# A feed-forward stage put in the order of its source: all engines by hand, gate sums on DVE, left sums two steps later, w3's sums over four steps

## The chip, the cores and the metric

The kernel runs on one core of a Trainium2 chip. The metric is device time in microseconds (us), the median of several executions. The engines are named as the profile names them: PE (TensorE), DVE (VectorE), ACT (ScalarE), POOL (GpSimd), SP (SyncE, which here issues the transfers). Each engine works through its own queue in order, and waits on semaphores for the others.

## The reference

The kernel computes one transformer layer in float32 for 16 sequences of 128 rows with 1024 features: cross-attention with a residual, and a gated feed-forward network (FFN) with a residual, each behind a layer norm. Cut to what matters:

```python
x = x + cross_attention(layernorm(x), ctx, mask)
xn = layernorm(x)
x12 = jnp.einsum('bsk,mk->bsm', xn, w12) + b12      # w12: 2048 x 1024
x1, x2 = jnp.split(x12, 2, axis=-1)
x4 = jax.nn.silu(x1) * x2
out = x + jnp.einsum('bsm,nm->bsn', x4, w3) + b3    # w3: 1024 x 1024
```

The kernel calls the residual stream `x1` (the `x` of the last line), and the gated product `h` (the `x4` here).

## The kernel before

Both products of the FFN are made with fewer multiplications than the plain form. The first product, F here, is a two-level seven-product scheme. The outer level splits the operands into 2 x 2 quarters and forms seven products, in the order `OUTER = (1, 2, 3, 6, 5, 7, 4)`; for each of them there are four groups g of rows of w12 (each holds gate rows and value rows), so that there are 28 *steps*, `STEPS = [(g, i) for i in OUTER for g in range(4)]`: i=1 is steps 0 to 3, i=2 steps 4 to 7, i=3 steps 8 to 11, i=6 steps 12 to 15, i=5 steps 16 to 19, i=7 steps 20 to 23 and i=4 steps 24 to 27. In each step the function `seven` does the inner level: seven inner products of four chunks each, in the order `INNER = (1, 5, 6, 7, 2, 3, 4)`, accumulated in PSUM. The second product, G, is a scheme of 26 products on 4 x 4 blocks (`bilinear`), done for four groups of columns, G0 to G3.

Each product needs sums made by other engines:

- *Outer sums.* `outer_sum` makes the left operand of outer products 5, 6, 3 and 7 on POOL from quarters of w12 (128 x 1024 elements each, lines L836, L839, L841, L845). A sum is kept in DRAM (`keep_sum`) and read back (`load_sum`) two steps ahead of its use.
- *Inner left sums.* `inner_left` makes four sums of 128 x 256 elements for each step on POOL, one step ahead (L289, tiles named L).
- *Right sums.* `outer_right` and `inner_right` make the sums of the right operand on DVE (128 x 1024 each, tiles X); `made` says at which step and product.
- *u1 and u3.* In each step ACT copies the first inner product out of PSUM (L271), and DVE adds it to the later ones (u1 at L274, u3 at L276). PE's inner product 3 adds to the bank that u3 reads, and product 4 to the bank of product 7, so PE waits there if DVE is late.
- *The state.* `done` adds each outer product to running sums u, v and w of each group, which are kept as two tiles of 128 x 1024 per group; `spill` and `unspill` move them to DRAM and back. When a block of the result is complete, `finish` puts it on the list `due`: gates get their silu on ACT (L901), values are multiplied with the gate on DVE (L895), and the product is stored to `hT_dram` by SP (L898). `settle_due` works off the list after each inner product.
- *For G.* `w3_R.advance` loads blocks of w3 and makes their sums on DVE in the last steps of F; `load_left` reads `hT` back, `load_x1` loads four tiles of x1 and b3, spread over all partitions; `add_b3` adds b3 to x1 on DVE (L1035).

What happens when is written out by hand as a plan: `at(n, j, fn, ...)` calls a function in step n after inner product j. In the kernel before, that plan fixes the order for PE only (`tc.manual_schedule(engines={PE})`); the order of the instructions on DVE, ACT, POOL and SP is chosen by the framework's scheduler from its own costs. All loads and stores are issued by SP, with at most eight outstanding: each one waits for the eighth before it. Large tiles share a pool of 44 units of 512 KB, smaller temporaries one of 14[...].

Of the kernel before, what the change touches and what calls it, by code (L numbers as in the profile page):

```python
# [15 lines left out]
AX = mybir.AxisListType  # L16
PSUM = bass.MemoryType.PSUM
# [100 lines left out]
def xattn_ffn_kernel(  # L118
# [33 lines left out]
    ctx.enter_context(tc.manual_schedule(engines={mybir.EngineType.PE}))  # L152
# [732 lines left out]

    gate, held, due = {}, {}, []
# [30 lines left out]
    def step(n):  # L917
        g, i = STEPS[n]

        def done(rc, s, ps):  # L920
# [8 lines left out]
            elif i == 2:  # L929
                t = temp([512], f"C11_{g}_{r}{c}")  # L930
                nc.vector.tensor_add(t, u, ps)
                if s is not None:
                    nc.gpsimd.tensor_add(t, t, s)
                finish(g, 0, 0, r, c, t)
            elif i == 6:
                nc.vector.tensor_add(u, u, ps)
                if s is not None:
                    nc.vector.tensor_add(u, u, s)
            elif i == 5:
                nc.vector.tensor_add(w, u, ps)  # L940
                if s is not None:
                    nc.vector.tensor_add(w, w, s)
                nc.gpsimd.tensor_add(v, v, w)
                finish(g, 0, 1, r, c, v)
            elif i == 7:
                if s is None:
                    nc.vector.tensor_add(w, w, ps)
                    nc.vector.tensor_add(u, u, ps)
                else:
                    t = temp([512], f"M7_{g}_{r}{c}")  # L950
                    nc.vector.tensor_add(t, s, ps)
                    nc.vector.tensor_add(w, w, t)
                    nc.gpsimd.tensor_add(u, u, t)
                finish(g, 1, 1, r, c, w)
            else:
                nc.vector.tensor_add(u, u, ps)
                if s is not None:
                    nc.gpsimd.tensor_add(u, u, s)
                finish(g, 1, 0, r, c, u)
# [7 lines left out]
    for n, (g, i) in enumerate(STEPS):  # L967
# [3 lines left out]
        else:  # L971
# [3 lines left out]
        if i == 1:  # L975
            at(n - (g > 0), 1 if g == 0 else 6, load_quarter, g, 1, 0)
            at(n - (g > 0), 2 if g == 0 else 7, load_quarter, g, 1, 1)
            at(n, 4 if g == 0 else 1, outer_sum, g, 5)
            at(n, 5 if g == 0 else 2, outer_sum, g, 6)
            for k in (5, 6):  # L980
                at(n + 1, 1, keep_sum, g, k)
        if i == 2:
            at(n - 2, 3, load_sum, g, 6)
            at(n, 1, outer_sum, g, 3)
            at(n + 1, 1, keep_sum, g, 3)
        if i == 6:
            at(n - 2, 3, load_quarter, g, 0, 0)
            at(n - 2, 4, load_quarter, g, 1, 0)
            at(n, 1, outer_sum, g, 7)
            at(n + 1, 1, keep_sum, g, 7)  # L990
# [6 lines left out]
        for k, s in ((6, "u"), (5, "v")):  # L997
            if i == k:
                at(n - 1, 2, unspill, g, s)
# [15 lines left out]
    made(5, [(4, 7), (5, 7), (6, 7), (7, 7)], sums((12, 3), (12, 6), (13, 4), (14, 4)))  # L1015
    made(6, [(7, 3), (8, 2), (8, 6), (9, 2)], sums((9, 5), (10, 2), (10, 5), (11, 2)))
    made(7, [(9, 7), (10, 7), (11, 4), (11, 6)], sums((16, 4), (17, 4), (18, 4), (19, 4)))
    made(4, [(13, 6), (14, 6), (15, 3), (15, 6)], sums((20, 4), (21, 4), (22, 4), (23, 4)))
# [15 lines left out]
    def add_b3(k, i):  # L1034
        nc.vector.tensor_add(x1_in[k][i], x1_in[k][i], last["b3"])  # L1035
# [29 lines left out]
    for j in range(1, 8):  # L1065
        for e in range(3):
            at(N - 3 + e, j, w3_R.advance, 7 * e + j)
    at(N - 3, 3, load_left, 0)
    at(N - 2, 2, load_x1, 0)
    for j in range(4):  # L1070
        at(N - 1, 1 + j, lambda j=j: A[0].advance(j))
        at(N - 1, 4 + j, add_b3, 0, j)
# [27 lines left out]
    stream.add(*(step(n) for n in range(N)))  # L1100
    stream.finish()
    settle_due()
# [63 lines left out]
```

## Time and profile before

| | |
|---|---|
| median of the runs | 1217.68 us (1216.41 to 1219.34, three runs) |
| profiled execution | 1217.48 us |
| its span | 1215.5 us |
| granted PE clock, mean | 0.986 |
| PE busy | 1167.4 us (96%) |
| DVE busy | 840.5 us (69%) |
| POOL busy | 678.1 us (56%) |
| ACT busy | 330.7 us (27%) |
| bytes moved | 183.86 MB, 151 GB/s over the span |

The span is the time between the first and the last instruction of the profiled execution; the 2 us around it belong to the launch. "Busy" is the time in which an engine had an instruction under way. The page divides the span into 40 slices of about 30 us and gives a digit for each. Queries of the trace give, for a stretch of time, the busy time of each engine, what each wait of an engine was for, and the groups of instructions with the same line and shape. F runs from about 647 us to 999 us, G to the end.

### The profile page before, as it was taken

To read this page: it belongs to the slowest core of one execution; us is meant where nothing else is said; L and a number is where in the kernel's file an instruction comes from. 1 tells how busy PE (TensorE), PEld (TensorE's weight loads), DVE (VectorE), ACT (ScalarE), POOL (GpSimd) and SP (SyncE) were. 2 spreads that over 40 slices of the span, in tenths; PEclk is the share of its full clock that TensorE was granted. 3 is DMA by queue.
4 is the path that set the end of the run, shared out by engine and by line. 5 is a ranking of instruction groups with operands and counts; after the bars stand their busy time and mean duration, and the time that the engine had idled before them with its cause. 6 is when DMAs were issued, how large, how long until landed. Compare 5 with 4: busy or idle time off the path is not lost.

```text
span 1215.5 us, 13386 instructions
## 1 busy us (share of the span) xinstructions
PE 1167.4 (96%) x4276; PEld 542.1 (45%) x4276; DVE 840.5 (69%) x1211; ACT 330.7 (27%) x1308; POOL 678.1 (56%) x584
## 2 busy tenths in 40 slices
PE   7999999999999999999999987999996998899998
PEld 3444445445444545444454433444442443344443
DVE  4742368977687888888343685647687769989762
ACT  0000044555445454544342211110011111111210
POOL 6753256745457556647153695537179455547645
PEclk9999999999999999999999998999998999899999
DMA  9535342221215513153576772368143351252411
GB/s 367 204 111 200 102 158 87 88 87 53 87 53 191 183 68 116 47 185 136 217 272 238 292 255 107 122 255 349 52 159 127 112 199 70 95 200 103 165 70 69
DMA packets 60900, 183.86 MB, mean 151 GB/s; under 512 B 6560, under 2 KB 10656, under 8 KB 60832
## 3 DMA queue, kind: packets, MB, share of 16 engines
q1 hardware_dynamic: 59248, 178.81, 40.3%
q10 hardware_dynamic: 1584, 4.21, 0.9%
q8 instruction: 34, 0.56, 0.2%
q14 instruction: 34, 0.28, 0.1%
HBM read 121.14 MB, written 61.87 MB: 151 GB/s over the span
## 4 chain that ended last, share of the span: by engine, by line
PE 80%; POOL 8%; DVE 6%; DMA 3%; issue 2%; ACT 1%; SPq 0%; POOLq 0%; DVEq 0%; ACTq 0%
PE F_b L187 21%; PE Q_b L187 18%; PE O_b L187 16%; PE G_b L187 14%; PE pt L547 4%; POOL L L289 3%; PE s L514 3%; PE o L559 2%; POOL A_S L289 2%; DMA b_sb<-in_b_dram 1%; POOL wm L436 1%; DVE w_R L289 1%; PE xt L653 1%; DMA S6r<-S_dram 1%; DVE wo_T L231 1%
## 5 line engine op out<-in xcount | busy, mean ns | idle before, releaser
L541 POOL TENSOR_TENSOR p<-p,inv 128x512 f32<-128x512 f32 x128 | 136.3, 1087 | 168.2 <-DVE inv L538 128.9
L532 ACT ACTIVATE p<-s,nmax 128x128 f32<-128x128 f32 x512 | 181.4, 406 | 176.2 <-DVE nmax L526 168.7
L187 PE MATMUL F_b<-X_T,L 128*128 128x512 f32 x304 | 137.5, 599 | 2.2 <-POOL L L289 2.2
L532 ACT ACTIVATION_READ_ACCUMULATOR p<-s,nmax 128x1 f32 x512 | 126.0, 246 | 0.0
L187 PE MATMUL G_b<-w_R,A_L 128*128 128x512 f32 x256 | 116.1, 598 | 6.4 <-DVE A_L L289 6.4
L523 DVE SCALAR_TENSOR_TENSOR s<-s,mr,drop 128x512 f32<-128x512 f32 x128 | 90.3, 750 | 24.9 <-PE s L514 24.9
L549 DVE COPY pT<-pt 128x512 f32<-128x512 f32 x128 | 84.3, 675 | 18.1 <-PE pt L547 17.6
L547 PEld LDWEIGHTS pt<-ident,p 128*128 128x128 f32 x512 | 63.6, 141 | 69.8 <-issue 63.7
L187 PEld LDWEIGHTS F_b<-X_T,L 128*128 128x128 f32 x304 | 57.8, 192 | 74.7 <-issue 66.6
L187 PE MATMUL F_b<-xnT,L 128*128 128x512 f32 x128 | 64.5, 623 | 18.6 <-DVE F_u L276 18.6
L526 DVE TENSOR_REDUCE nmax<-s 128x4 f32<-128x512 f32 x128 | 81.7, 678 | 0.0
L187 PEld LDWEIGHTS G_b<-w_R,A_L 128*128 128x128 f32 x256 | 49.1, 192 | 68.8 <-issue 67.1
L547 PE MATMUL pt<-ident,p 128*128 128x128 f32 x512 | 76.9, 273 | 2.4 <-issue 2.4
L289 POOL TENSOR_TENSOR x<-x,G_n 128x512 f32<-128x512 f32 x36 | 51.5, 1454 | 39.2 <-DVE G_n L352 18.3
L289 POOL TENSOR_TENSOR x<-x,G_c 128x512 f32<-128x512 f32 x36 | 53.9, 1511 | 34.7 <-ACT G_c L370 30.4
L370 ACT COPY G_c<-G_b 128x512 f32<-128x512 f32 x52 | 30.3, 585 | 143.3 <-PE G_b L187 130.7
L187 PE MATMUL O_b<-wo_T,O_S 128*128 128x512 f32 x128 | 61.7, 601 | 0.0
L187 PE MATMUL O_b<-wo,O_S 128*128 128x512 f32 x128 | 61.6, 601 | 0.0
L187 PE MATMUL Q_b<-xT,wq 128*128 128x512 f32 x128 | 60.0, 596 | 0.0
L187 PE MATMUL Q_b<-xT_T,A_S 128*128 128x512 f32 x128 | 59.9, 598 | 0.0
L187 PE MATMUL Q_b<-xT,A_S 128*128 128x512 f32 x128 | 59.7, 598 | 0.0
L187 PE MATMUL O_b<-wo,OTr 128*128 128x512 f32 x112 | 55.6, 601 | 0.2 <-DMA OTr<-OT_dram 0.2
(220 smaller groups left out, 2091.5 us busy)
## 6 DMA issues: line engine op xcount, KB each, us to landing
w<-in_w_dram SPq DMA_DIRECT2D x36, 512.0 KB, 5.5
xT<-in_xT_dram SPq DMA_DIRECT2D x16, 512.0 KB, 6.7
xs<-in_x_dram SPq DMA_DIRECT2D x16, 512.0 KB, 6.0
xp<-in_x_dram SPq DMA_DIRECT2D x16, 512.0 KB, 6.6
x_dram<-xp SPq DMA_DIRECT2D x16, 512.0 KB, 2.6
xn_dram<-xn SPq DMA_DIRECT2D x16, 512.0 KB, 2.9
xnr<-xn_dram SPq DMA_DIRECT2D x16, 512.0 KB, 5.8
h<-hT_dram SPq DMA_DIRECT2D x16, 512.0 KB, 4.4
```

What stands on the lines that cost most here:

```text
L187: nc.tensor.matmul(ps, lhsT, rhs, start=start and i == 0, stop=stop and i == len(pairs) - 1, skip_group_check=True,)
L231: eng.tensor_sub(t[e], a()[e], b()[e])
L289: (eng.tensor_add if op == "+" else eng.tensor_sub)(out, a, b)
L370: nc.scalar.copy(t, ps)
L514: nc.tensor.matmul(ps[gl][:, j, :], QT[T, c, gh * 2 + j // 2][rows, j % 2, toks], KT[T, c][rows, gh, toks], start=True, stop=True,)
L523: nc.vector.scalar_tensor_tensor(s, s, rstd, drop.unsqueeze(1).to_broadcast([P, HPG, S]), ALU.mult, ALU.add,)
L526: nc.vector.tensor_reduce(nmax[:, e], s, AX.X, ALU.max, negate=True)
L532: nc.scalar.activation(p[:, j, :], ps[gl][:, j, :], AF.Exp, bias=nmax[:, e, j : j + 1], accum_out=total[:, e, j : j + 1],)
L541: nc.gpsimd.tensor_mul(p, p, inv[:, e].unsqueeze(2).to_broadcast([P, HPG, S]))
L547: nc.tensor.transpose(pt[:, j, :], p[:, j, :], ident)
L549: nc.vector.tensor_copy(pT, pt)
L559: nc.tensor.matmul(o[ds(gl * DH, DH), :, :], V[T, c][:, i, ts(gh * GL + gl, DH)], pTs[gl], start=True, stop=True,)
```

## The change

Six things change, all in F or at its border with G.

1. Inside F, the order of the source holds for all five engines instead of PE alone. Outside it nothing changes.
2. For i=2, the sum of the inner result and the gate's running sum (`C11`) is added on DVE instead of POOL.
3. Outer sums 5 and 6 are made two steps after their group's step of i=1 instead of in it, from quarters loaded one step after it. Outer sum 3 is made two steps ahead of its step of i=3, from sum 6 and a quarter loaded for it, and outer sum 7 two steps ahead of its step of i=7; neither goes through DRAM any more.
4. For i=5, w and v are formed from the product alone on DVE (one of the four blocks of w by a copy on ACT), and POOL adds u to the whole tiles of v (one step before) and of w (one step after); v is read back one step earlier.
5. The sums of the right operand for i=5, 6, 7 and 4 are made at other steps and products.
6. The first 20 of w3's blocks and sums are spread over four steps, five in each, instead of three with seven. x1 and b3 are loaded in step 25 after product 5 instead of step 26 after product 2, and for the first group of columns POOL adds b3 in step 26 instead of DVE in step 27.

```diff
+    def add_u(g, s):
+        for r in range(2):
+            nc.gpsimd.tensor_add(state[g, s][r], state[g, s][r], state[g, "u"][r])
...
                 nc.vector.tensor_add(t, u, ps)
                 if s is not None:
-                    nc.gpsimd.tensor_add(t, t, s)
+                    nc.vector.tensor_add(t, t, s)
                 finish(g, 0, 0, r, c, t)
...
             elif i == 5:
-                nc.vector.tensor_add(w, u, ps)
-                if s is not None:
-                    nc.vector.tensor_add(w, w, s)
-                nc.gpsimd.tensor_add(v, v, w)
+                if s is None:
+                    nc.vector.tensor_add(v, v, ps)
+                    nc.scalar.copy(w, ps)
+                else:
+                    nc.vector.tensor_add(w, s, ps)
+                    nc.vector.tensor_add(v, v, w)
                 finish(g, 0, 1, r, c, v)
...
         if i in (1, 2, 4):
             at(n - 2, 2, load_quarter, g, i // 2 // 2, (i + 1) // 3)
-        else:
+        elif i in (6, 5):
             at(n - 2, 2, load_sum, g, i)
...
         if i == 1:
-            at(n - (g > 0), 1 if g == 0 else 6, load_quarter, g, 1, 0)
-            at(n - (g > 0), 2 if g == 0 else 7, load_quarter, g, 1, 1)
-            at(n, 4 if g == 0 else 1, outer_sum, g, 5)
-            at(n, 5 if g == 0 else 2, outer_sum, g, 6)
+            for e, (R, K) in enumerate(((1, 0), (1, 1), (0, 0))):
+                at(n + 1, 4 + e, load_quarter, g, R, K)
+            at(n + 2, 2, outer_sum, g, 5)
+            at(n + 2, 3, outer_sum, g, 6)
             for k in (5, 6):
-                at(n + 1, 1, keep_sum, g, k)
-        if i == 2:
-            at(n - 2, 3, load_sum, g, 6)
-            at(n, 1, outer_sum, g, 3)
-            at(n + 1, 1, keep_sum, g, 3)
-        if i == 6:
-            at(n - 2, 3, load_quarter, g, 0, 0)
-            at(n - 2, 4, load_quarter, g, 1, 0)
-            at(n, 1, outer_sum, g, 7)
-            at(n + 1, 1, keep_sum, g, 7)
+                at(n + 3, 1, keep_sum, g, k)
+        if i == 3:
+            at(n - 3, 2, load_quarter, g, 0, 1)
+            at(n - 3, 3, load_sum, g, 6)
+            at(n - 2, 1, outer_sum, g, 3)
+        if i == 7:
+            at(n - 3, 2, load_quarter, g, 0, 0)
+            at(n - 3, 3, load_quarter, g, 1, 0)
+            at(n - 2, 1, outer_sum, g, 7)
...
-                at(n - 1, 2, unspill, g, s)
+                at(n - 1 - (k == 5), 2, unspill, g, s)
+        if i == 5:
+            at(n - 1, 2, add_u, g, "v")
+            at(n + 1, 3, add_u, g, "w")
...
-    made(5, [(4, 7), (5, 7), (6, 7), (7, 7)], sums((12, 3), (12, 6), (13, 4), (14, 4)))
-    made(6, [(7, 3), (8, 2), (8, 6), (9, 2)], sums((9, 5), (10, 2), (10, 5), (11, 2)))
-    made(7, [(9, 7), (10, 7), (11, 4), (11, 6)], sums((16, 4), (17, 4), (18, 4), (19, 4)))
-    made(4, [(13, 6), (14, 6), (15, 3), (15, 6)], sums((20, 4), (21, 4), (22, 4), (23, 4)))
+    made(5, [(8, 1), (8, 3), (8, 5), (8, 7)], sums((12, 3), (13, 3), (14, 3), (15, 3)))
+    made(6, [(9, 2), (9, 4), (9, 6), (10, 1)], sums((10, 3), (10, 6), (11, 2), (11, 4)))
+    made(7, [(16, 2), (16, 5), (17, 2), (17, 5)], sums((18, 2), (18, 5), (19, 2), (19, 5)))
+    made(4, [(12, 6), (13, 6), (14, 6), (15, 6)], sums((20, 4), (21, 4), (22, 4), (23, 4)))
...
     def add_b3(k, i):
-        nc.vector.tensor_add(x1_in[k][i], x1_in[k][i], last["b3"])
+        (nc.vector if k else nc.gpsimd).tensor_add(x1_in[k][i], x1_in[k][i], last["b3"])
...
-    for j in range(1, 8):
-        for e in range(3):
-            at(N - 3 + e, j, w3_R.advance, 7 * e + j)
+    for e in range(4):
+        for j in range(1, 6):
+            at(N - 4 + e, j, w3_R.advance, 5 * e + j)
+    at(N - 1, 6, w3_R.advance, 21)
     at(N - 3, 3, load_left, 0)
-    at(N - 2, 2, load_x1, 0)
+    at(N - 3, 5, load_x1, 0)
     for j in range(4):
+        at(N - 2, 2 + j, add_b3, 0, j)
         at(N - 1, 1 + j, lambda j=j: A[0].advance(j))
-        at(N - 1, 4 + j, add_b3, 0, j)
...
-    stream.add(*(step(n) for n in range(N)))
-    stream.finish()
-    settle_due()
+    with tc.manual_schedule(engines={ENGINES.PE, ENGINES.DVE, ENGINES.Activation, ENGINES.Pool, ENGINES.SP}):
+        stream.add(*(step(n) for n in range(N)))
+        stream.finish()
+        settle_due()
```

## The prediction

> **What bounds the kernel now.** I read the page's first two parts, then PE's waits inside the FFN, then busy time by stage, then the groups of POOL, then the transfer of b3.
>
> ```profile
> PE 1167.4 (96%) x4276; PEld 542.1 (45%) x4276; DVE 840.5 (69%) x1211; ACT 330.7 (27%) x1308; POOL 678.1 (56%) x584
> ...
> PE   7999999999999999999999987999996998899998
> ...
> PEclk9999999999999999999999998999998999899999
> ```
>
> PE is busy 96% of the span, so only its 48 us of idle time, and the slower clock behind it, can be won. The dents are in the first slices (loads, untouched) and in three places of the FFN's first product, slices 24, 31 and 34. PE's waits from 640 to 1045 us (line, what it waited for, total, times, longest):
>
> ```profile
> PE F_b L187 <- DVE F_u L276: 18.6, 4, 9.6
> PE G_b L187 <- DVE A_L L289: 6.4, 1, 6.4
> PE F_b L187 <- ACT F_p L271: 4.2, 1, 4.2
> PE F_b L187 <- POOL L L289: 2.2, 1, 2.2
> PE F_b L187 <- DVE ur L956: 0.6, 1, 0.6
> ```
>
> Their sum is 32.1 us. The stretches that hold them, and an undisturbed one (columns: PE, PEld, DVE, ACT, POOL busy, granted clock, DMA share, GB/s):
>
> ```profile
> 700.00:750.00 50.00, 36.94 (x74) 14.72 (x73) 35.54 (x31) 6.66 (x12) 40.92 (x30) 0.86 0.58 209
> 750.00:800.00 50.00, 50.00 (x118) 22.08 (x117) 29.52 (x35) 6.39 (x10) 21.60 (x19) 1.00 0.33 122
> ...
> 900.00:950.00 50.00, 40.39 (x91) 17.66 (x90) 37.95 (x43) 7.37 (x11) 40.15 (x36) 0.90 0.40 137
> ...
> 1000.00:1050.00 50.00, 41.16 (x93) 17.80 (x92) 47.20 (x58) 7.83 (x13) 28.02 (x16) 0.93 0.27 98
> ```
>
> Undisturbed, 118 matmuls take 50 us, 0.4237 each. At that rate 74, 91 and 93 would take 31.4, 38.6 and 39.4 us; busy were 36.94, 40.39 and 41.16: 5.6 + 1.8 + 1.8 = 9.2 us go to the lower clock after the gaps. So these places lose 32.1 + 9.2 = **41 us**. In the first two windows POOL is at 82% and 80% (43% in the undisturbed one); in the third DVE is at 94%. The POOL groups, 640 to 1040 us (busy us, mean ns):
>
> ```profile
> L289 POOL TENSOR_TENSOR L<-w 128x256 f32<-128x256 f32 x22 | 24.1, 1113 | 0.0
> L943 POOL TENSOR_TENSOR vr<-vr,w 128x512 f32<-128x512 f32 x16 | 23.0, 1450 | 34.7 <-PE F_b L187 27.6 <-DVE w L942 7.1
> ...
> L933 POOL TENSOR_TENSOR C<-C,F_u 128x512 f32<-128x512 f32 x12 | 16.0, 1340 | 23.0 <-DVE C L931 23.0
> ...
> L841 POOL TENSOR_TENSOR S6r<-w,S6r 128x1024 f32<-128x1024 f32 x4 | 10.4, 2589 | 1.0 <-issue 1.0
> L839 POOL TENSOR_TENSOR w<-w,w 128x1024 f32<-128x1024 f32 x4 | 10.3, 2569 | 0.3
> ```
>
> The reader is to see POOL's prices: a left sum 0.72 us alone (its minimum), 1.1 mean; 128x512 1.26 alone, 1.34 to 1.71 mean; 128x1024 2.35 alone, 2.4 to 2.6 mean, 3.22 at most. In 700 to 750 it does twelve left sums for i=2, four S6r sums and six C11 adds at once, and PE waits for what follows. At 922 the gating product (L895) on DVE waits for a POOL add of L943 that stands behind eight left sums of i=7; u1 and u3 stand behind it on DVE, and PE waits 9.6 us for u3. At 1021 and 1032 DVE is late: 21 sums of w3 in three steps and four adds of b3.
>
> **The change part by part.** I count t from PE's first F matmul (647.4 us): a step takes 12.02 us undisturbed, 13.77 in steps 0 to 3 with their turns, so step k from 4 on starts at 55.1 + 12.02(k-4), the second product G at 343.5.
>
> *Steps 0 to 9.* The outer sums 5 and 6 go two steps later, each by its own loads of three quarters, sum 3 to i=3's steps, and the C11 adds (12 x 1.34 = 16.0 us) leave POOL for DVE (12 x 0.94, the mean of DVE's 128x512 adds there, = 11.3 us, 2.8 a step). In steps 4 to 7 (48 us) POOL now has four outer sums (9.8), two sums 3 (4.9) and 24 left sums (26.5 at 1.1): 41 us, in the order in which PE asks for them: the last outer sum ahead of the left sums of step 5 ends near t=54, they are wanted at 68.8. Four X5 blocks (128x1024, 1.2 to 2.4 us) leave DVE in steps 4 to 7 for step 8, which pays for its adds. I take the whole 13.1 + 5.6 = 18.7 us of the first stall as gone. If POOL's cover failed, up to those 18.7 would stay.
>
> *Transfers.* S3 and S7 are no longer written and read: 16 fewer of 512 KB, 8 more loads of quarters. SP's list is 8 shorter. The queue is at 122 to 209 GB/s there; cost nothing, covered by two steps of lead.
>
> *Steps 15 to 23.* Per group POOL loses four L943 adds (4 x 1.26 = 5.0 us alone) and gets four 128x1024 adds of u (4 x 2.35 = 9.4). Sum 7 stays; w starts as an ACT copy (0.58 us, on an engine busy 6.7 of 50 us), and v is read back a step earlier, which holds two buffers longer: nothing, as loads wait for no buffer there. POOL is now the tight engine. w += u of group 0 waits for the end of step 16 (t=211) and ends at 216; its sum 7 waits for loads that stand in SP's queue behind a store of hT for which DVE is done near 214: six loads and two stores, 3.5 MB at 370 GB/s, t=224. From there to the first left sum of step 21 (wanted t=261.1) POOL has eleven 128x1024, nine left sums and one 128x512: alone 25.9 + 6.5 + 1.3 = 33.6, ready at 258; at the means 11 x 2.5 + 9 x 1.05 + 1.5 = 38.5, ready at 262.5; with waits between, up to 264. Late by 0 to 3 us, then kept through step 22. I take **+3**. The 9.6 + 1.8 us of the old stall go: v no longer gets its last add from POOL, so the gating product behind it waits for DVE's own adds.
>
> Here a rule speaks against the change. The row: beside a DVE that is 71% busy, 128x1024 on POOL took 2.59 instead of 2.35, 10% more, and a left sum 1.1 instead of 0.72. The Trainium skill, "Trainium Architecture — The Big Picture", section "What this means for kernel authors", says that DVE and GpSimd share a port pair, and "it's an exclusive lock (not a bandwidth split)". Taken in full, POOL would stand still for each DVE instruction with two operands in SBUF. In steps 16 to 19 these are per step three adds (0.94), two gating products (about 1) and two X sums (1.3): 7.4 of 12 us. 33.6 us of POOL work would then take 33.6 / 0.38 = 88 us, 50 us late, and the kernel would be slower. The rows show nothing near this for the large adds, so I use the means; the rule keeps the upper end open.
>
> *Steps 24 to 27 and G's start.* w3's sums go over four steps (5 a step instead of 7), and four adds of b3 leave DVE: 4 x 1.5 = 6 us and some five sums of 1.3 us less in the window where DVE was at 94%. I take the 0.6 + 2.4 + 6.4 + 1.8 = 11.2 us there as gone. But the adds of b3 go to POOL at step 26, between group 2's last left sums and those of step 27:
>
> ```profile
> L1035 DVE TENSOR_TENSOR x<-x,b_sb x4: 1209/1280/2284, 1002.4 to 1034.8; 128x1024 f32<-128x1024 f32 x4
> ...
> DMA to landing us min/median/max: 9.1/9.1/9.1
> ```
>
> b3 landed 9.1 us after its issue, at 1002.4 (the add's first start), 12.7 us behind the hT stores of step 24 with six more loads ahead of it. In the changed program SP's list has twelve loads ahead of it behind those stores (three of w3, step 27's quarter, four of h, four of x1). The stores wait for DVE, as before 4.4 us after step 24 ends (t=307.5): t=312. 13 x 0.52 MB + 0.5 = 7.3 MB at the 350 to 400 GB/s of that burst is 18 to 21 us, with some 2 us to land t=332 to 335; I take 334. Behind it POOL has a b3 add twice, a 128x512, left sum 5, b3, left sum 6, b3, a 128x512, left sum 7: 4 x 2.35 + 2 x 1.26 + 3 x 0.72 = 14.1 us, ready at 348 alone and 350 at the means; PE wants left sum 7 at 336.7. **A new stall of 11 to 14 us**, taken as 13, with 1.8 for the clock as after the 9.6 gap. Queued behind it: POOL's adds of step 26, and DVE's gating products, which wait for them and have u1 of step 27 behind them (about 1 more). DVE makes w3's sums meanwhile, so G starts without another wait.
>
> *Source order.* No row shows what it does elsewhere. Lower bound nothing, or a gain of the under 1 us of small waits; upper bound one wait like those of the scheduler's order, 4 us. Taken as 1.
>
> Sum, against the profiled execution's own 1217.48 us (span 1215.5 and 2 around; 0.2 below the median of the runs): 1217.5 - 18.7 - 11.4 - 11.2 = 1176.2; + 3 + 13 + 1.8 + 1 + 1 = **1196 us**.
>
> **The rivals.**
> *b3 costs nothing*: if b3 lands by t=322, as it would with half the burst ahead of it, the left sums are in time. For it: in the trace's transfers from 985 to 1005 us single half-microseconds reach 459 GB/s. Against: twelve loads can't land in 10 us. Between 1177 and 1188, likeliest 1181. Chance 0.25.
> *POOL too slow, moderately*: the middle between means and maxima in steps 16 to 22, 12 us, or an order on DVE or SP that blocks as much: 1203 to 1214. Chance 0.15.
> *POOL is the bound and the kernel is slower*: with the maxima (3.22, 1.77, 2.31) the same list takes 35.4 + 15.9 + 2.3 = 53.6 from t=224: 16.5 late at step 21, 5 more at step 22, 2 at 23, and three gaps at 1.8: 29 us for my 3, 1222. It decides from about 24 us late, nearly the maxima throughout, or half of the lock. For it: DVE gets two-input adds in the same steps. Against: the means. Chance 0.12.
> *Nothing moves*: gains and stalls cancel within 0.2% (2.4 us, about what a measurement of this kernel tells from no change). Chance 0.03.
>
> **How the numbers follow.** The case of the sum has 0.45 (1189 to 1203 by its own bounds). Range 1179 to 1214: the sum's case, most of the b3 rival, the moderate one. Faster 0.45 + 0.25 + 0.15 = 0.85, of which I give 0.01 to slower: 0.84, same 0.03, slower 0.13.
>
> **What would show it.** Right: no wait of PE for F_u or F_p in steps 4 to 5; granted clock 1.00 there; POOL's adds of u at 2.4 to 2.6 us; a wait of 11 to 14 us in step 27 for POOL's L with b3's landing ahead of it; no wait of G for A_L. Wrong: waits for L in steps 20 to 22 over 5 us (POOL), b3 landing within 12 us of the hT stores, or waits of PE for DVE that stands behind ACT, POOL or a load by the new order.

## The result: no gain, and a new set of stalls in place of the old

The changed kernel takes 1220.05 us in the median of 20 runs (1216.84 to 1223.4), the kernel before 1218.94 in 20 runs beside it (1216.22 to 1220.9). The ratio is 1.0015, interval 1.0005 to 1.0025: slower by about 0.15%, less than the 0.2% that the prediction counted as no change. The forecast was 1196, with a range of 1179 to 1214. The profiled execution took 1222.38 us (span 1220.6), 4.9 more than that of before. It lies 2.3 us above its kernel's median and that of before 1.5 below, so the two traces differ by more than the medians do; 1.1 us of their difference is there before F starts (648.5 us instead of 647.4), where the change touches nothing.

PE's waits of the changed kernel from 640 to 1060 us, in the columns of the prediction's second fence:

```profile
PE F_b L188 <- DVE F_u L277: 12.8, 5, 4.4
PE F_b L188 <- POOL L L290: 12.5, 4, 5.4
PE G_b L188 <- DVE A_L L290: 4.5, 1, 4.5
PE F_b L188 <- DVE ur L963: 0.2, 1, 0.2
```

They sum to 30.0 us, against 32.1 before. Busy time by stretch (PE, PEld, DVE, ACT, POOL, granted clock, DMA share, GB/s):

```profile
700.00:750.00 50.00, 50.00 (x124) 22.64 (x123) 35.25 (x45) 9.95 (x17) 25.31 (x21) 1.00 0.65 243
...
850.00:900.00 50.00, 42.00 (x91) 17.92 (x90) 45.74 (x43) 7.77 (x13) 34.77 (x18) 0.93 0.34 123
900.00:950.00 50.00, 46.84 (x105) 20.25 (x104) 47.54 (x46) 7.07 (x11) 43.43 (x28) 0.96 0.19 67
950.00:1000.00 50.00, 42.58 (x90) 18.17 (x89) 33.12 (x38) 7.05 (x11) 30.32 (x25) 0.90 0.55 204
1000.00:1050.00 50.00, 38.67 (x78) 15.74 (x77) 39.16 (x47) 6.55 (x11) 29.78 (x18) 0.90 0.30 111
```

The first row is the stall of steps 4 and 5 that the change removes in full: PE is busy all 50 us at full clock, and POOL has gone from 40.9 to 25.3 us. It is given back, and more, from 850 us on, in four stretches where only two were disturbed before. By the prediction's own rate (0.4237 us a matmul) 91, 105, 90 and 78 matmuls take 38.6, 44.5, 38.1 and 33.1 us; busy were 42.0, 46.8, 42.6 and 38.7: the clock takes 3.4 + 2.3 + 4.4 + 5.6 = 15.7 us, where 9.2 were lost before. (Some records are missing, so this is good to a few us; counted from the granted clock in rows of 1 us, where PE is busy, it is 13.4 us against 8.0.) Waits and clock together, by the prediction's way of counting: 45.7 us now, 41.3 before.

Three waits start the new stalls. They are seen in the timeline of the changed kernel (start, us, engine, line, tiles; in brackets how long the engine had been idle, and for what). At the border of steps 17 and 18 POOL stands at outer sum 7, and adds of u stand behind it:

```profile
865.46 2.83 DVE L900 SCALAR_TENSOR_TENSOR vr<-vr,b_sb,vr 128x512 f32<-128x512 f32 x1
...
868.32 0.32 SPq L903 DMA_DIRECT2D hT_dram<-vr  x1
...
870.12 0.92 SPq L182 DMA_DIRECT2D w<-in_w_dram  x2
...
878.52 3.44 POOL L846 TENSOR_TENSOR w<-w,w 128x1024 f32<-128x1024 f32 x1 [6.62 <-DMA w<-in_w_dram]
```

The two quarters were issued at 870.1, behind a store of hT that waited for DVE: the gating product (L900) took 2.83 us, while POOL added u, where it takes 0.74 alone. In step 24 and again in step 25 DVE stands at a sum of w3:

```profile
965.93 1.96 SPq L903 DMA_DIRECT2D hT_dram<-w  x2
...
967.98 2.32 SPq L182 DMA_DIRECT2D w<-in_w_dram  x5
...
977.28 1.23 DVE L290 TENSOR_TENSOR w_R<-w,w 128x1024 f32<-128x1024 f32 x1 [6.99 <-DMA w<-in_w_dram]
979.18 1.26 POOL L965 TENSOR_TENSOR ur<-ur,F_u 128x512 f32<-128x512 f32 x1 [6.87 <-DVE ur L963]
...
981.18 2.77 PE L188 MATMUL F_b<-xnT,L 128*128 128x512 f32 x4 [3.04 <-POOL L L290]
...
988.25 1.22 DVE L290 TENSOR_TENSOR w_R<-w,w 128x1024 f32<-128x1024 f32 x1 [4.22 <-DMA w<-in_w_dram]
```

Here one late transfer stops four engines in turn: SP issues w3's blocks behind stores, DVE waits 6.99 us for one, its adds of u come after it, POOL waits 6.87 us for such an add with the left sums behind it, and PE waits for a left sum. The plan calls for the sum one inner product, 1.7 us, after the load; the scheduler of before was free to put other work ahead. The third wait is b3's:

```profile
L1044 POOL TENSOR_TENSOR x<-x,b_sb x4: 2332/2388/3333, 1005.4 to 1017.0; 128x1024 f32<-128x1024 f32 x4
...
DMA to landing us min/median/max: 10.7/10.7/10.7
```

It landed at 1005.3, 22.4 us after the stores of step 24 that stand ahead in SP's queue (982.9).

### The profile page after: what moved, and what is told of

The parts are those of the page before. It is cut to its first block, busy times and chain, and to the rows that moved or that the text cites. A ratio compares the mean times of both kernels' runs of the same rounds, so it can differ in the third digit from the quotient of the medians.

```text
span 1220.6 us, 13378 instructions
## 1 busy us (share of the span) xinstructions
PE 1173.1 (96%) x4276; PEld 543.5 (45%) x4276; DVE 862.5 (71%) x1219; ACT 332.4 (27%) x1312; POOL 690.6 (57%) x576
## 4 chain that ended last, share of the span: by engine, by line
PE 81%; DVE 7%; POOL 5%; DMA 4%; issue 2%; ACT 0%; SPq 0%; DVEq 0%; POOLq 0%; ACTq 0%
PE F_b L188 21%; PE Q_b L188 18%; PE O_b L188 16%; PE G_b L188 14%; PE pt L548 4%; PE s L515 3%; PE o L560 2%; DMA w<-in_w_dram 2%; POOL A_S L290 2%; DMA b_sb<-in_b_dram 1%; PE xt L654 1%; POOL wm L437 1%; POOL x L1044 1%; POOL ur L965 1%; DVE wo_T L232 1%
## 5 line engine op out<-in xcount | busy, mean ns | idle before, releaser
L188 PE MATMUL F_b<-X_T,L 128*128 128x512 f32 x304 | 141.7, 614 | 8.7 <-POOL L L290 8.7
L188 PE MATMUL F_b<-xnT,L 128*128 128x512 f32 x128 | 64.6, 623 | 16.5 <-DVE F_u L277 12.8
L188 PE MATMUL F_b<-xnT,w 128*128 128x512 f32 x128 | 61.1, 600 | 0.0
```

Of the source, the lines that this page charges most:

```text
L188: nc.tensor.matmul(ps, lhsT, rhs, start=start and i == 0, stop=stop and i == len(pairs) - 1, skip_group_check=True,)
```

## The experiments

Theory A: in the source's order an engine stops at the first instruction whose data are late, and what stops here are late *transfers*. Theory B: the moved work is simply too much for POOL and DVE. Later, theory C: POOL's 128x1024 adds and DVE's adds with two operands in SBUF hold each other up; and D: where within a step a long DVE sum stands matters. Ratios are to the kernel before, run beside each, with 95% intervals. Differences in us are of medians, which can stray from the ratios by 1 to 2 us (e1 gains 11.6 us by the medians, 13.5 by the ratios).

| run | edit on the changed kernel | us | ratio |
|---|---|---|---|
| (the change) | | 1220.05 | 1.0015 (1.0005 to 1.0025) |
| e1 | w3 loads early | 1208.47 | 0.9904 (0.9886 to 0.9922) |
| e2 | quarters of sum 7 early | 1224.42 | 1.0038 (1.0023 to 1.0053) |
| e3 | b3 as before | 1217.41 | 0.9979 (0.9970 to 0.9988) |
| e4 | PE alone in source order | 1216.69 | 0.9974 (0.9965 to 0.9983) |
| e5 | e1, i=5 as before | 1206.12 | 0.9891 (0.9878 to 0.9904) |
| e6 | e1, X7 sums in steps 10, 11 | 1208.61 | 0.9905 (0.9890 to 0.9920) |
| e7 | e1, x1 and b3 loaded early | 1209.46 | 0.9913 (0.9897 to 0.9930) |
| e8 | kernel before, all engines in source order | 1224.48 | 1.0039 (1.0026 to 1.0053) |
| e9 | e1, b3 added inside G0 | 1200.92 | 0.9858 (0.9838 to 0.9879) |
| e10 | e1, sums of X7 and w3 late in the step | 1211.81 | 0.9949 (0.9931 to 0.9967) |
| e11 | e10, i=5 as before, b3 inside G0 | 1195.77 | 0.9818 (0.9797 to 0.9839) |
| e12 | e13, quarters of sum 7 early | 1204.74 | 0.9887 (0.9867 to 0.9907) |
| e13 | e10, b3 inside G0 | 1203.23 | 0.9867 (0.9848 to 0.9886) |
| e14 | e11, w3 sums back at products 1 to 5 | 1194.25 | 0.9797 (0.9778 to 0.9816) |
| e15 | e14, quarters of sum 7 early | 1193.45 | 0.9791 (0.9771 to 0.9811) |
| e16 | e14, PE alone in source order | 1210.62 | 0.9921 (0.9899 to 0.9944) |

### e1: w3's loads early

```diff
-    w3_R = Right(lambda q, c: load(w3[q, c], [2, 512], f"w3_{q}_{c}"), "w3")
+    w3_in = {}
+
+    def load_w3(q, c):
+        w3_in[q, c] = load(w3[q, c], [2, 512], f"w3_{q}_{c}")
+
+    w3_R = Right(lambda q, c: w3_in[q, c], "w3")
...
+    for e, qc in enumerate(((2, 1), (2, 0), (0, 1), (3, 1))):
+        at(N - 5, 1 + e, load_w3, *qc)
+    for n, j, qc in ((N - 4, 1, (0, 0)), (N - 4, 3, (1, 0)), (N - 4, 5, (3, 0)), (N - 2, 1, (1, 1))):
+        at(n, j, load_w3, *qc)
```

> The eight loads of w3's blocks are issued a step or more ahead (four in step 23, three in step 24, one in step 26) instead of one product ahead of the sum that reads them. Theory A (in source order DVE stands still on a sum of w3 whose load is late, and u1, the adds of u and POOL's adds and left sums stand behind it): DVE's waits of 7.0 us at 970 and 4.2 us at 984 go, and with them PE's 3.0 (POOL L) and 4.4 (DVE F_u) and the 4.4 us that the lower clock costs there: about 10 us faster, 1209 to 1212 us. Theory B (POOL's and DVE's work itself is too much there, through contention): PE's waits in steps 24 and 25 stay or move, within 3 us of the changed kernel, 1217 to 1221.

Measured: 1208.47 us, 11.6 less than the changed kernel: theory A, and not B, in step 25. PE's waits from 640 to 1060 us:

```profile
PE F_b L188 <- POOL L L290: 13.0, 6, 4.8
PE F_b L188 <- DVE F_u L277: 5.5, 4, 2.6
PE G_b L188 <- DVE A_L L290: 2.3, 1, 2.3
```

Those for F_u fell from 12.8 to 5.5; the waits of 3.0 and 4.4 us in step 25 are gone but for 0.3. Those for L did not fall in sum: step 27, which PE now reaches earlier, waits 4.8 and 1.8 us for left sums behind b3, where it waited 3.3 and 0.7.

### e2: the quarters of sum 7 early

```diff
-            at(n - 3, 2, load_quarter, g, 0, 0)
-            at(n - 3, 3, load_quarter, g, 1, 0)
+            at(n - 4, 2, load_quarter, g, 0, 0)
+            at(n - 4, 3, load_quarter, g, 1, 0)
```

> The two quarters for outer sum 7 are loaded four steps ahead of their step of i=7 instead of three; nothing else. Theory A (POOL stands still on a late load, with ready adds of u behind it): POOL's wait of 6.6 us at 872 goes, PE's wait of 5.4 us for POOL L at 888 goes, and of the 3.2 us at 916 most; with 3 to 5 us of clock 8 to 12 us faster, 1208 to 1212. Theory B (POOL has more work than time because its 128x1024 adds take 2.8 to 3.4 us beside DVE): the time won is used up by the adds, PE waits in step 21 or 22 instead, gain 0 to 4 us, 1216 to 1220.

Measured: 1224.42 us, slower, which neither theory had. PE's wait for L at the start of step 19 (5.4 us) is gone, but close by it waits 7.0 us for F_u. Just ahead of u1 two gating products (L900) take 5.57 us beside two adds of u. What changed is how long DVE's instructions take. In the trace of the changed kernel, 840 to 945 us (min/median/max, ns):

```profile
L949 DVE TENSOR_TENSOR w<-F_u,F_b x12: 673/679/689, 857.3 to 909.1; 128x512 f32<-128x512 f32 x12
...
L950 DVE TENSOR_TENSOR vr<-vr,w x12: 692/1576/2811, 858.1 to 909.8; 128x512 f32<-128x512 f32 x12
...
L889 POOL TENSOR_TENSOR w<-w,ur x8: 2347/2786/3321, 862.0 to 914.7; 128x1024 f32<-128x1024 f32 x8
```

and in e2:

```profile
L950 DVE TENSOR_TENSOR vr<-vr,w x12: 691/2127/2591, 859.4 to 914.5; 128x512 f32<-128x512 f32 x12
```

L949 and L950 have one shape. L949 reads a PSUM bank (F_b) and never takes over 0.69 us; L950 reads two tiles in SBUF and takes up to 2.8 us, four times its price. POOL's adds stretch from 2.35 to 3.3. The reading was that POOL's idle 6.6 us had kept the two apart, and that once it is filled DVE is late instead. This made theory C, which the later runs test.

### e3: b3 as before

```diff
-        (nc.vector if k else nc.gpsimd).tensor_add(x1_in[k][i], x1_in[k][i], last["b3"])
+        nc.vector.tensor_add(x1_in[k][i], x1_in[k][i], last["b3"])
...
-    at(N - 3, 5, load_x1, 0)
+    at(N - 2, 2, load_x1, 0)
...
-        at(N - 2, 2 + j, add_b3, 0, j)
         at(N - 1, 1 + j, lambda j=j: A[0].advance(j))
+        at(N - 1, 4 + j, add_b3, 0, j)
```

> x1 and b3 are loaded in step 26 and b3 is added on DVE in step 27, as before the change; the rest is the changed kernel. Theory A (b3's landing holds POOL's left sums of step 27): PE's waits of 3.3, 0.7 and 2.6 us in step 27 go, and DVE, with 6 us more in step 27, makes PE wait 3 to 6 us more at G's start: in all 0 to 6 us faster, 1214 to 1220. Rival (the left sums of step 27 are late for another reason, the adds of u that wait for DVE): the waits for POOL L stay and DVE is later: 2 to 6 us slower, 1222 to 1226.

Measured: 1217.41 us, 2.6 less than the changed kernel. PE waits for no left sum in step 27 any more, so b3 was their cause; but G's start waits 9.0 us instead of 4.5, more than expected.

### e4: PE alone in source order

```diff
-    with tc.manual_schedule(engines={ENGINES.PE, ENGINES.DVE, ENGINES.Activation, ENGINES.Pool, ENGINES.SP}):
+    with tc.manual_schedule(engines={ENGINES.PE}):
```

> The changed kernel with only PE held to the source's order, as before the change; all other edits stay. Theory A (the source's order costs by blocking queues on late loads): the scheduler puts other work ahead of what waits, most of the 30 us of PE's waits in steps 16 to 27 goes: 1195 to 1210. Theory B (the moved work costs, whatever the order): within 5 us of the changed kernel, 1215 to 1225. A third case: the scheduler bunches work as before the change, stalls come in other steps, 1210 to 1230.

Measured: 1216.69 us, 3.4 less than the changed kernel. The time lies in the ranges of theory B and of the third case, and the waits are the third case's. PE waits 28.3 us in all, in other places: 4.5 us in steps 4 to 7, a single wait of 8.1 us for ACT near the end of F. The scheduler avoids the late loads and makes stalls of its own; by this run alone the source's order would be a loss.

### e5: i=5 as before, on e1

```diff
-                if s is None:
-                    nc.vector.tensor_add(v, v, ps)
-                    nc.scalar.copy(w, ps)
-                else:
-                    nc.vector.tensor_add(w, s, ps)
-                    nc.vector.tensor_add(v, v, w)
+                nc.vector.tensor_add(w, u, ps)
+                if s is not None:
+                    nc.vector.tensor_add(w, w, s)
+                nc.gpsimd.tensor_add(v, v, w)
...
-        if i == 5:
-            at(n - 1, 2, add_u, g, "v")
-            at(n + 1, 3, add_u, g, "w")
```

> The early w3 loads of the first experiment, and i=5 as before the change (POOL adds w to v in four 128x512, no adds of u to whole tiles). Theory C (in steps 16 to 22 POOL's 128x1024 adds and DVE's adds with both operands in SBUF hold each other up): POOL's load there falls by 4.4 us a group, DVE's adds come back from a median of 1.2 to 1.6 us to about 0.7, PE's waits of 0.7, 1.9, 4.8 and 1.1 us there go with some 3.5 us of clock: 6 to 11 us faster than the first experiment, 1198 to 1203. Rival (the late load in SP's queue is what counts, not the adds): POOL still waits 6 us for the quarters of sum 7, and the 4.8 us wait stays: 1206 to 1210.

Measured: 1206.12 us, only 2.4 less than e1, at the rival's edge; yet the 4.8 us wait for L in step 19 that the rival kept is gone. In its place PE waits 3.9 us for F_u in step 18: an X sum of 128x1024 for i=7 that stands ahead of u1 took 3.36 us beside POOL's sum 7. So both halves of the reading were incomplete; the place of the X sums was the next suspect.

### e6: the sums of i=7 early, on e1

```diff
-    made(7, [(16, 2), (16, 5), (17, 2), (17, 5)], sums((18, 2), (18, 5), (19, 2), (19, 5)))
+    made(7, [(10, 4), (10, 5), (11, 3), (11, 5)], sums((18, 2), (18, 5), (19, 2), (19, 5)))
```

> The early w3 loads, and the four sums of the right operand for i=7 in steps 10 and 11 as about before the change, instead of steps 16 and 17; POOL's adds of u stay. Theory C: DVE has two sums of 128x1024 less in each of steps 16 and 17, that is 5 to 8 us less beside POOL's adds; PE's 1.9 us wait for DVE F_u goes, the wait for POOL L falls by 1 to 3 us: 2 to 6 us faster than the first experiment, 1203 to 1207. Rival (late load alone): 1207 to 1210.

Measured: 1208.61 us, as e1 and in the rival's range. The wait of 1.9 us for F_u in step 17 went, as theory C had it, but PE then waited 5.1 us for L in step 19, as POOL was still held by the quarters. One cause taken away while its neighbour stays gives nothing.

### e7: x1 and b3 loaded early, on e1

```diff
-        if k == 0:
-            last["b3"] = load(b3.partition_broadcast(P), [D], "b3_sb")
...
+    at(N - 5, 6, lambda: last.update(b3=load(b3.partition_broadcast(P), [D], "b3_sb")))
-    at(N - 3, 5, load_x1, 0)
+    at(N - 4, 6, load_x1, 0)
```

> The early w3 loads, and b3 loaded in step 23 and x1 in step 24 instead of both in step 25; POOL still adds b3 in step 26. Theory A (b3's late landing holds POOL's left sums): PE's waits of 4.8 and 1.8 us for POOL L in step 27 go, with some 3 us of clock: 5 to 10 us faster than the first experiment, 1199 to 1204. Rival (the four adds of 2.35 us themselves and the adds of u in between are too much): a wait of 3 to 5 us for POOL L stays: 1205 to 1209.

Measured: 1209.46 us, as e1. That is the rival's time, but not its sign: the landing no longer holds anything, and the waits for L in step 27 fell from 6.6 to 1.7 us. But the timeline of e7 shows what takes their place:

```profile
987.35 6.07 POOL L1042 TENSOR_TENSOR x<-x,b_sb 128x1024 f32<-128x1024 f32 x2
987.85 3.37 DVE L290 TENSOR_TENSOR w_R<-w,w 128x1024 f32<-128x1024 f32 x1
991.25 3.25 DVE L290 TENSOR_TENSOR w_R<-w,w_R 128x1024 f32<-128x1024 f32 x1
994.42 0.68 DVE L275 TENSOR_TENSOR F_u<-F_b,F_p 128x512 f32<-128x512 f32 x1
...
995.97 2.05 PE L188 MATMUL F_b<-xnT,L 128*128 128x512 f32 x2 [4.48 <-DVE F_u L277]
```

Two adds of b3 on POOL start with two sums of w3 on DVE; each sum takes 3.3 us where it takes 1.2 alone, u1 comes 4.2 us later for it, and PE waits 4.48 us. The four instructions take turns: alone they are 2 x 2.35 + 2 x 1.21 = 7.1 us, and from the start of the first (987.35) to the end of the last (994.50) it is 7.15. This is e2 again at another place.

### e8: the kernel before, all engines in source order

```diff
-    stream.add(*(step(n) for n in range(N)))
-    stream.finish()
-    settle_due()
+    E = mybir.EngineType
+    with tc.manual_schedule(engines={E.PE, E.DVE, E.Activation, E.Pool, E.SP}):
+        stream.add(*(step(n) for n in range(N)))
+        stream.finish()
+        settle_due()
```

> The kernel before, with all five engines in the source's order in the first product and no other edit. Theory A (the order blocks queues on late loads and late adds, so the old plan, written for a scheduler, must suffer): PE waits more in steps 0 to 8 and 16 to 27, 10 to 60 us slower than before, 1230 to 1280. Rival (the order is harmless by itself): within 5 us of before, 1214 to 1224.

Measured: 1224.48 us, about 5 more than before: less than theory A's bound, just over the rival's. PE's waits from 640 to 1060 us:

```profile
PE F_b L187 <- DVE F_u L276: 16.9, 9, 4.9
PE F_b L187 <- POOL L L289: 7.6, 1, 7.6
PE G_b L187 <- DVE A_L L289: 6.6, 1, 6.6
```

Those from 700 to 800 us fall from 13.1 to 6.6 us by the order alone, the 9.6 us wait in step 20 falls to under 1, and PE waits 22.6 us from step 24 on (7.6, 3.5, 4.9 and 6.6 us), where the old plan too asks for w3's sums soon after their loads. So the order alone, with i=5 in its old form, removes the stall of step 20.

### e9: b3 added inside G0, on e1

```diff
-        (nc.vector if k else nc.gpsimd).tensor_add(x1_in[k][i], x1_in[k][i], last["b3"])
+        nc.vector.tensor_add(x1_in[k][i], x1_in[k][i], last["b3"])
...
+            if k == 0 and i in (8, 10, 12, 14):
+                add_b3(0, i // 2 - 4)
...
-        at(N - 2, 2 + j, add_b3, 0, j)
```

> The early w3 loads, and b3 added on DVE inside G0 (after products 8, 10, 12 and 14) instead of on POOL in step 26; its loads stay in step 25. Neither b3's landing nor the collision of POOL's 128x1024 adds with DVE's sums can hold step 27. Theory C (both prices stand on those four adds: the landing in the first experiment, the collision in the run with b3 early): PE's waits for POOL L (4.8, 1.8) and for F_u (2.6) in step 27 go, G's start waits at most 4 us, G0 pays nothing: 8 to 13 us faster than the first experiment, 1196 to 1201. Rival (DVE is short of time there anyway, so that the wait only moves to G's start or into G0): 1204 to 1209.

Measured: 1200.92 us, 7.6 less than e1, at the upper end of theory C's range. Where e7 removed only the landing and gained nothing, taking POOL's adds out of steps 26 and 27 removes landing and collision. The waits for L there are down to 0.2, and G's start waits 2.8.

### e10: the sums of i=7 and w3 late in the step, on e1

```diff
-            at(N - 4 + e, j, w3_R.advance, 5 * e + j)
-    at(N - 1, 6, w3_R.advance, 21)
+            at(N - 4 + e, j + 2, w3_R.advance, 5 * e + j)
+    at(N - 1, 7, w3_R.advance, 21)
...
-    made(7, [(16, 2), (16, 5), (17, 2), (17, 5)], sums((18, 2), (18, 5), (19, 2), (19, 5)))
+    made(7, [(16, 4), (16, 6), (17, 4), (17, 6)], sums((18, 4), (18, 6), (19, 4), (19, 6)))
```

> The early w3 loads; and the sums of the right operand for i=7 and of w3 come after u1 and u3 in each step (products 3 to 7 of the plan instead of 1 to 5), so that in DVE's order they no longer stand between the last step's adds and u1. Theory D (place within a step: a long sum ahead of u1 holds PE): the waits for F_u of 1.9 us in step 17 and 2.6 us in step 27 go, 2 to 5 us faster than the first experiment, 1203 to 1207, if G's start loses no more than 2. Theory C alone (the collisions, wherever they are): the waits stay or move, 1207 to 1211.

Measured: 1211.81 us, about 3 more than e1: a miss for theory D, and 0.8 over theory C's range. The wait of 1.9 us in step 17 went, that of 2.6 in step 27 stayed, G's start waits 6.0 us instead of 2.3, as w3's last sums are later, and PE waits 6.7 us for L and 5.4 for F_u in steps 19 and 20. With POOL's adds of u there, moving DVE's sums only moves the collision.

### e11 and e13: with and without POOL's adds of u

e11 is e10 with the edits of e5 and e9, e13 is e10 with that of e9 alone; they differ only in the form of i=5.

> All that helped in one: early w3 loads, late sums, i=5 as before the change, b3 inside G0. Theory C with D: PE's waits from step 16 on fall to under 8 us: 1190 to 1198. If POOL's and DVE's collisions are not what is left: 1199 to 1206.

> Early w3 loads, late sums and b3 inside G0 as in e11, but with the changed form of i=5 (POOL's adds of u to whole tiles). Theory C (adds of u and DVE's adds with both operands in SBUF hold each other up): PE's waits of 5 to 12 us in steps 16 to 21 are there, and DVE's adds there have a median over 1.2 us: 7 to 12 us slower than e11, 1203 to 1208. Rival (the form of i=5 hardly matters once the sums are placed late): within 3 us of e11, 1195 to 1199.

Measured: 1195.77 and 1203.23 us, in two sessions; by the ratios 0.9818 and 0.9867 the adds of u cost about 6 us, by the medians 7.5, where theory C had 7 to 12; the intervals do not meet. In the trace of e13 PE waits 0.8 and 6.4 us for L and 4.2 for F_u in steps 17 to 20:

```profile
PE F_b L188 <- POOL L L290: 7.2, 2, 6.4
PE F_b L188 <- DVE F_u L277: 6.0, 2, 4.2
PE G_b L188 <- DVE A_L L290: 6.0, 1, 6.0
```

e11 has only waits of up to 0.6 there:

```profile
PE G_b L188 <- DVE A_L L290: 6.0, 1, 6.0
PE F_b L188 <- DVE F_u L277: 4.2, 5, 1.8
PE F_b L188 <- POOL L L290: 2.8, 7, 0.5
```

With the sums late, i=5's old form is worth some three times what it was in e5. The median of L950 in e13 was 1.17 us, just below the 1.2 expected.

### e12: the quarters early, with the adds of u

e13 with the edit of e2.

> Early w3 loads, late sums, b3 inside G0, the adds of u on POOL kept, and the quarters of outer sum 7 loaded a step earlier (the edit that alone made it slower). Theory D: with the sums of i=7 out of the way of u1, the earlier load gives what it should have given, the wait of 4.8 us for POOL L in step 19 goes: 1194 to 1200. Theory C: POOL's adds of u then run all the time beside DVE, DVE's adds with both operands in SBUF take over 2 us, PE waits 5 us or more for F_u in steps 17 to 20: 1201 to 1207, slower than the run before.

Measured: 1204.74 us (0.9887), against 0.9867 for e13; the intervals overlap. Theory C's time holds, but not its signs: PE waits for L (6.6 and 1.7 us) more than for F_u (3.6), and the median of L950 is 1.04 us. POOL's adds of u, at 2.8 us each, are late by themselves. So part of what they cost is POOL's own work, as theory B had it (4.4 us a group by its prices alone); how much of the 6 to 7.5 us is that, and how much the collisions, these runs do not part.

### e14, e15, e16: the best version, and two questions to it

e14 is e11 with w3's sums at products 1 to 5 again; e15 adds the edit of e2 to it, e16 that of e4.

> e11 with w3's sums back at products 1 to 5 of each step (their loads stay early; the sums for i=7 stay late). Theory D holds for i=7 only: G's start waits 3 us instead of 6, step 27 waits 2 us for F_u as in e9: 1190 to 1194.5. Rival (the 6 us at G's start come from the last gating products, which wait for POOL and ACT): 1195 to 1198.

> e14 with the quarters of outer sum 7 loaded a step earlier. Theory C: without the adds of u the earlier load collides with nothing much: within 2 us of e14. Rival (the earlier load itself hurts, by its transfers or by SP's order): 3 to 6 us slower than e14, as it was in the changed kernel.

> e14 with only PE held to the source's order. Theory A (the order costs only through late loads, which e14 has mended; beyond that the scheduler's order bunches work): 5 to 20 us slower than e14, 1197 to 1212. Rival (the scheduler's order is the better one in general): 1180 to 1190.

Measured: 1194.25, 1193.45 and 1210.62 us, in one session, each in the range of the theory named first. e14 beats the kernel before by 2.0% (0.9797, 0.9778 to 0.9816) and PE's waits are 10.0 us in all:

```profile
PE F_b L188 <- DVE F_u L277: 4.7, 6, 1.9
PE F_b L188 <- POOL L L290: 3.0, 8, 0.5
PE G_b L188 <- DVE A_L L290: 2.3, 1, 2.3
```

e15 is the same within its interval: the early quarters, which went with a loss in e2, cost nothing once the adds of u are gone. And e16 answers what e4 could not: with the late loads, b3 and i=5 mended, the source's order is worth 16 us; which of the three mends it needs, no run shows. In e16 the scheduler's order brings PE's waits of 2.8 us back to step 4, and 3.7, 4.0 and 2.0 us to the steps around 21.

## Why the prediction was wrong, point by point

Two terms carry most of the miss: "Source order", put at 1 us, failed in its mechanism and came at 11.8; POOL in steps 15 to 23, put at 3, was mis-sized and came at 17.

*Steps 0 to 9: right.* 18.7 us were to go, and the row 700 to 750 shows all of them gone. The prediction put this down to POOL's moved work alone. It took both halves of the change: e4 has the edits without the order and keeps 4.5 us of waits there, e8 has the order without the edits and keeps 6.6 of 13.1.

*The old stall in step 20: the right number for the wrong reason.* The 9.6 us wait for the gating product is gone. The prediction credited i=5's new form, in which v no longer gets its last add from POOL. But e8, e11 and e14 keep the old form in the source's order and wait at most 0.6 us there, and e16, with the old form in the scheduler's order, has waits of 3.7 and 4.0 us. It was the order that removed it, and that this term came out was luck.

*POOL in steps 15 to 23, "+3": mis-sized.* The waits there are 0.7, 1.9, 5.4 and 3.2 us, 11.2 in all, with 5.7 of clock; 5.4 were for POOL's left sums and 5.8 for DVE. The quarters of sum 7 landed at t=230, where 224 was forecast: the way from DVE's product to the landing took 10.2 us for 10, but the product was done at t=219.8 instead of 214. POOL then had its adds at 2.8, not 2.5 us. And the sum priced a collision by what it adds to *POOL's* instruction and left *DVE's* out. The trace of before had the sign (840 to 950 us; L942 has both operands in SBUF, L940 one in PSUM, and the shape is the same):

```profile
L942 DVE TENSOR_TENSOR w<-w,F_u 128x512 f32<-128x512 f32 x12 | 11.3, 942 | 0.2
L940 DVE TENSOR_TENSOR w<-ur,F_b 128x512 f32<-128x512 f32 x16 | 10.8, 680 | 2.0 <-PE F_b L187 2.0
```

The lock that the prediction set aside was right in kind: in e7 a DVE sum and a POOL add take turns, one instruction at a time. What was wrong is the 50 us made of it, in which POOL always gave way. In turns POOL loses one DVE instruction an add (2.35 becomes 2.8, at most 3.4), and DVE a whole POOL add, up to four times its price, ahead of u1 and u3. The Trainium skill, "GPSIMD Engine Reference", section "8. Key points", names two kinds of DVE instruction that contend, those in a 2-port mode and those with two SBUF inputs; L949 and L950 agree with the second. By e11 and e13 the adds of u cost 6 to 7.5 us, clock included.

*"Source order, taken as 1", upper end 4: the step whose mechanism failed.* The new plan's w3 sums follow their loads by one product, and in the source's order DVE and then POOL, ACT and PE stand still behind each. That is 3.0 + 4.4 us of waits and 4.4 of clock in the row 950 to 1000, all in step 25; e1, which moves only the loads, gains 11.6 us. The prediction called the w3 edit a gain on DVE's load, and never set the distance from a load to its sum against the time that loads take in the trace of before (medians of 3.6 us for blocks of w and 6.6 for x1 from 975 to 1030 us, and the 9.1 of b3 that it shows itself). A wait of PE for DVE that stands behind a load was one of its own signs of being wrong.

*b3: the mechanism right, the size wrong by half.* b3 was to land 22 us after the stores of step 24, and landed 22.4 after. Behind it POOL worked in the order that was forecast and had left sum 7 ready 15.8 us later, for 14 to 16. But PE waits 3.3 + 0.7 us for left sums in step 27 and not 13: held up by the stalls in step 25, it started step 27 at 1008.9 and would have come to left sum 7 three products later, some 8.7 us after the landing, not 2.7. It waits 2.6 us for DVE, for about 1, of which e3 keeps 1.8 without b3 on POOL; and 4.5 us at G's start were not expected. e7 shows that the landing is only half of it: with b3 there in time, its adds collide with w3's sums.

*The clock: 1.8 us where the four stretches lost 15.7.* The sum charged it once. The waits came as eleven of 0.2 to 5.4 us, in four places; six of them were followed by a slow clock, and each place had at least one.

*The sum.* The losses of before, 41 us, were all that could be won; 19.8 were expected in their place, 45.7 came: about 17 in steps 15 to 23 and 11.8 in step 25, with the clock, 6.6 in step 27 and 4.5 at G's start, and 5.6 of clock behind these two. In the median the kernel is 1.1 us slower.

*The rivals.* "POOL too slow, moderately" named both causes, but as alternatives for 12 us in all: POOL's times halfway between means and maxima, or an order on DVE or SP that blocks. Both came, and the time went past its 1214. The slower rival named the right engines and the wrong victim: POOL's times were not at their maxima, and the kernel was slower all the same, by loads. The rival that nothing moves has the measured time, by chance: gains and losses of 40 us cancel.

## What to carry to other kernels

When an order chosen by a scheduler is replaced by one written by hand, go through every load and ask how far ahead of its first reader it stands, and what else stands behind that reader on its engine; here one product of 1.7 us stood against 7 us of waiting, and that cost 11.6 us. With this, b3 and the adds of u mended, the order is a gain of 16 us. When work goes to POOL, price it on DVE too: each DVE instruction with both operands in SBUF that falls beside it gets longer, and it is DVE's place ahead of the critical result that decides. Where two causes hold the same stage, taking one away shows nothing (e2, e6, e7), so try them together before calling either harmless.

## What the runs showed of the hardware

In all eighteen traces, from 640 to 1060 us, DVE's 128x512 adds with one operand in PSUM took 0.67 to 0.69 us, whatever POOL did; those with both in SBUF took up to 2.85, and 128x1024 sums 1.21 to 3.38, while POOL's own 128x1024 adds went from 2.33 to 3.44. The two engines take turns, as the lines of e7 show.

And a short gap can cost clock. In e14 the only wait from 1000 to 1050 us is the 2.3 us at G's start; in steps of 2 us (the columns of the stretches above):

```profile
1010.00:1012.00 2.00, 0.12 (x1) 0.00 (x0) 2.00 (x2) 0.58 (x1) 0.82 (x1) 1.00 0.58 176
1012.00:1014.00 2.00, 1.62 (x2) 0.81 (x3) 2.00 (x7) 0.00 (x0) 0.00 (x0) 0.60 1.02 370
1014.00:1016.00 2.00, 2.00 (x4) 0.80 (x3) 2.00 (x5) 0.00 (x0) 0.00 (x0) 0.54 0.99 354
1016.00:1018.00 2.00, 2.00 (x6) 0.82 (x5) 2.00 (x3) 0.80 (x2) 1.21 (x1) 1.00 0.72 277
```

The clock is full when the wait begins and falls to half as work resumes, for 3.4 us, so that a wait of 2.3 us costs some 1.6 us more. Yet a longer wait can cost none. In the trace of before PE waits 3.1 us from 715.4 on, and the clock stays:

```profile
714.00:716.00 2.00, 1.43 (x4) 0.36 (x2) 2.00 (x3) 0.00 (x0) 2.00 (x2) 1.00 1.02 418
716.00:718.00 2.00, 0.00 (x0) 0.00 (x0) 2.00 (x4) 0.00 (x0) 1.92 (x2) 1.00 0.85 346
718.00:720.00 2.00, 1.45 (x4) 0.77 (x5) 1.59 (x3) 0.37 (x1) 2.00 (x4) 1.00 0.02 8
```

The granted clock in rows of half a microsecond shows why. The eighteen traces have 59 slow spells from 640 to 1060 us, each 3.41 us long or two, three or four times that. In each trace their starts lie on one grid of 3.41 us: in the changed kernel at 893.49, 920.80, 982.24, 989.07, 1012.96 and 1043.68, which are 8, 18, 2, 7 and 9 such steps apart. With that grid laid over the traces, a full clock fell to half after every step in which PE was idle for more than 2.0 us and after none with less than 1.9, and a half clock came back only after a step with at most 0.6 us of idle time. So what counts is how the wait falls on the grid: the 2.3 us of e14 lie in one step, and the 3.1 us of before on both sides of a mark. The Trainium skill, "TensorE: Matmul & The Clock Gate", section "What's actually happening", puts the fall after at least one idle window of about 3.4 us; here 1.9 to 2.0 us idle in one such step were enough, and the measurement decides. The seven waits of up to 0.6 us between 850 and 900 us in e14 leave the clock at 1.00 there.

A long wait also takes much of its slow spell into itself: the waits of 9.6 and 6.4 us of before cost 1.6 and 1.4 us of clock, while those of 5.4, 4.4 and 3.3 us of the changed kernel cost 3.0, 2.5 and 2.8. So waits of middle length can cost more than one long one of the same sum, which is where the change lost on the clock.
